# Pinning VectorE, ScalarE and GpSimd to the written order in attention and router, cutting the router into pieces, and splitting a prologue in two

## The chip, the cores and the metric

The kernel runs on one core of a Trainium2 chip. The core has five engines that work side by side, each with its own queue that it works off strictly in order: TensorE (PE in the profile; its weight loads are listed as PEld), VectorE (DVE), ScalarE (ACT), GpSimd (POOL) and SyncE (SP, which here only starts DMAs). [...] The metric is the time of one launch on the device in microseconds (us); lower is better.

## What is computed

One transformer layer over 2048 tokens of width 256, in float32: multi-head causal attention with rotated keys and queries, a residual and a layer norm, then a mixture of 16 experts (top 2) plus a shared expert, a residual and a second layer norm.

```python
q = (x @ Wq)                       # 16 heads of 16: 4 plain dims, 12 rotated by position
c_kv = x @ Wkv_down                # 64 wide
k, v = c_kv @ Wk_up, c_kv @ Wv_up  # k rotated like q
scores = where(causal, -inf, q @ k.T / 4)
x = layernorm(x + softmax(scores) @ v)
p = softmax(x @ gate_w.T);  weights, indices = top_k(p, 2)
y = sum over experts e of swiglu(x, w1[e], w3[e], w2[e]) * weight_of(e)
z = swiglu(x, sw1, sw3, sw2)       # the shared expert
out = layernorm(x + y + z)
```

## The kernel before

The tokens are cut into four chunks `c` of 512, the heads into four groups `g` of four. The name `g, c` stands for the queries of one chunk in one group.

**Attention is done in two passes.** The maxima pass (class `Maxima`) multiplies queries by keys, tile by tile, only to find each query's largest score: four matmuls per step, one a head (tiles `m`), which VectorE reduces to maxima (`pm`, lines 485 and 490). When all of `g, c` is through, `negated` (line 492) makes the tile `nm`: GpSimd fills it with zeros (line 494), VectorE writes the negated maxima into one column of 32 (line 495). `shift` (line 500) lets TensorE transpose `nm` into `pn`, and VectorE adds it to the queries, giving `qa`. The value pass (class `Weighted`) multiplies keys by `qa` (tiles `s`), ScalarE takes exponentials into `p` (line 535), GpSimd zeroes the upper triangle of diagonal tiles by an affine select (line 539), and TensorE multiplies by the values (`av`, one bank). The sums over key blocks are collected in `avs`: ScalarE copies `av` to `more` (line 566) and GpSimd adds it (line 567), or, in steps without a maxima part, VectorE adds it straight from PSUM (line 563).

**A plan written by hand sets the order.** The list `steps` pairs a maxima step with a value step; the main loop (from line 716) issues per step: two heads of `s`, two of `m`, their exponentials and reductions, then the other two heads of each, then the `av` matmuls of the step before, and then whatever `put(step, ...)` hung on this step: projections of keys, queries and values (`pk`, `pq`, `pv`), `negated` and two steps later `shift`, `finish` (line 569: divide, add to the residual, statistics), and for the last group the router. The last 20 value steps have no maxima part.

**The router of a chunk** is `normed` (layer norm, an inverse root of 12 small VectorE operations and four scalings), `turned` (transposes `pt`, copies to `xT`), `choose` (logits `lg`, softmax, top 2), `settle` (the place of each token in its expert's room, from two matmuls `pc`) and `scatter` (eight indirect DMAs, line 278, each issued by GpSimd). For the chunks 3, 0 and 1 they hang on steps at the end of attention; chunk `LAST` (2) is routed after it, between the shared expert's matmuls, and then the expert blocks follow.

**`prologue(c)`** transposes a chunk of x, copies it to `xT` and computes the latent `ckv` (`pc`) in one go; for the chunks 2 and 3 it hangs on the steps 3 and 7. `double(g)` (line 336) hangs on step 5 for g = 1 to 3: nine small copies on GpSimd, which wait for DMAs of weights (`wks`, `sines`).

**What sets an engine's order.** A scheduler at build time orders each engine's instructions by priority and readiness, by its own model of time, and may move an instruction ahead of earlier written ones. Only instructions handed to `tc.keep_in_program_order` keep the written order; before the change these are the matmuls and transposes, by the helper `pe` (line 136), and a few DMAs.

## Time and profile before

| what | value |
|---|---|
| median of 3 runs | 811.31 us (810.15 to 811.82) |
| the profiled execution, as timed | 803.1 us |
| its span, first to last instruction | 801.1 us |
| mean granted TensorE clock | 0.993 |
| busy: PE, DVE, ACT, POOL | 771.5, 547.1, 445.0, 323.0 us |
| attention with both passes | about 160 to 535 us of the span |
| last 20 value steps with three routers | about 535 to 595 us |
| shared expert, expert blocks, combination | from 595 us |

The page is read so: an engine's busy time is the union of its instructions; a matmul's end is modelled, so a busy PE says little, while the starts of matmuls are measured. In the timeline each row is a run of like instructions: start, length, engine, line, what is written and read, how many, and in brackets the idle time of the engine before it and what ended it. Every matmul of float32 has two records, a transpose one. All PE instructions stand under line 140, the helper's line, so they are told apart by their tiles.

### The profile page before, as it was taken

The page shows a single profiled execution, that of the slowest core. Times are in us where ns is not written, and L with a number is a line of the kernel's source. Part 1 is how long each engine was busy: PE and PEld are TensorE (multiplying, and loading weights), DVE is VectorE, ACT ScalarE, POOL GpSimd, SP SyncE. Part 2 cuts the span into 40 slices and gives each one's busy share as a digit, 9 for nine tenths or more (in the row PEclk, how much of TensorE's full clock was granted, in tenths as well). Part 3 has the DMA queues.
Part 4 walks back from the last instruction along what each step waited for, and adds up shares of the span by engine and source line. Part 5 has one row for each costly group of instructions (what it writes and reads, how often), then busy time and mean ns, then how long its engine had stood idle before and what let it go on. Part 6 is the DMA issues. An engine that isn't in the chain of part 4 may idle for free. (4 is left out here: it accounts for less than half of the span.)

```text
span 801.1 us, 14999 instructions
## 1 busy us (share of the span) xinstructions
PE 771.5 (96%) x5086; PEld 361.3 (45%) x5086; DVE 547.1 (68%) x1489; ACT 445.0 (56%) x997; POOL 323.0 (40%) x557
## 2 busy tenths in 40 slices
PE   7999999999999999999999999999989899999985
PEld 3443433444333344543334453444336466666543
DVE  2768888887687887777788678788775433333276
ACT  1143646377775786766688668875742033333345
POOL 2032524434355454635455454461661333333300
PEclk9999999999999999999999999999999999999998
DMA  5469999991000000001000000000225322222172
GB/s 147 130 174 327 310 301 304 294 301 54 2 1 1 1 2 1 2 19 37 1 2 2 1 2 2 1 2 2 80 84 141 107 80 86 82 86 70 37 230 85
DMA packets 67378, 71.88 MB, mean 90 GB/s; under 512 B 4736, under 2 KB 61539, under 8 KB 67302
## 3 DMA queue, kind: packets, MB, share of 16 engines
q1 hardware_dynamic: 62286, 61.77, 27.7%
q0 software_dynamic: 3552, 8.43, 3.0%
q10 hardware_dynamic: 1464, 0.72, 0.4%
q8 instruction: 41, 0.67, 0.4%
q14 instruction: 35, 0.29, 0.1%
HBM read 26.44 MB, written 45.78 MB: 90 GB/s over the span
## 5 line engine op out<-in xcount | busy, mean ns | idle before, releaser
L535 ACT ACTIVATE p<-s 128x512 f32<-128x512 f32 (+3 forms) x640 | 292.6, 540 | 128.2 <-PE m L140 79.0
L140 PE MATMUL m<-k,q 32*128 32x512 f32 (+3 forms) x1280 | 303.9, 566 | 0.8 <-DVE rot L423 0.5
L140 PE MATMUL s<-qa,k 32*128 32x512 f32 (+3 forms) x1280 | 279.4, 556 | 1.8 <-DVE avs L563 0.7
L490 DVE TENSOR_REDUCE pm<-m 128x1 f32<-128x512 f32 x384 | 237.5, 681 | 44.4 <-PE m L140 44.0
L567 POOL TENSOR_TENSOR avs<-avs,more 128x512 f32<-128x512 f32 (+3 forms) x125 | 136.7, 1094 | 167.3 <-ACT more L566 163.8
L140 PEld LDWEIGHTS s<-qa,k 32*128 32x128 f32 x1280 | 107.1, 184 | 117.6 <-ACT p L535 67.6
L140 PE MATMUL av<-p,v 128*32 128x512 f32 (+3 forms) x1280 | 154.2, 540 | 1.9 <-DVE base L244 1.2
L140 PEld LDWEIGHTS m<-k,q 32*128 32x128 f32 x1280 | 122.7, 184 | 44.5 <-issue 11.9
L485 DVE CUSTOM_DVE_ANT_0 m<-m,qmask 128x512 f32<-128x512 f32 (+3 forms) x256 | 118.3, 521 | 29.1 <-PE m L140 26.1
L566 ACT COPY more<-av 128x512 f32<-128x512 f32 (+3 forms) x125 | 65.6, 525 | 38.3 <-PE av L140 30.4
L539 POOL TENSOR_SCALAR_AFFINE_SELECT p<-p 128x128 f32<-128x128 f32 x256 | 70.5, 297 | 38.2 <-ACT p L535 36.4
L931 POOL DMA_INDIRECT yg<-yb,to x42 | 41.4, 985 | 88.2 <-ACT yb L923 44.1
L140 PEld LDWEIGHTS av<-p,v 128*32 128x32 f32 x1280 | 27.1, 108 | 104.1 <-ACT p L535 54.2
L140 PE MATMUL ph<-w,xbT 128*128 x168 | 60.3, 482 | 2.4 <-DVE xbT L884 1.7
L903 DVE TENSOR_TENSOR rh<-ru,ph 128x176 f32<-128x176 f32 x42 | 14.2, 338 | 53.7 <-ACT ru L901 53.7
L140 PE MATMUL h<-xT,cs 128*128 128x512 f32 (+1 forms) x96 | 43.6, 599 | 4.9 <-DVE sh L794 2.0
L901 ACT ACTIVATE ru<-ph 128x176 f32<-128x176 f32 x42 | 13.3, 318 | 59.3 <-PE ph L140 59.3
L140 PE MATMUL py<-w2r,hT 88*128 x168 | 43.4, 380 | 0.7 <-ACT hT L910 0.7
L278 POOL DMA_INDIRECT xg<-xr,slot x32 | 31.1, 971 | 31.1 <-issue 19.8
L140 PEld LDWEIGHTS ph<-w,xbT 128*128 128x128 f32 x168 | 28.5, 189 | 20.8 <-issue 11.6
L428 POOL TENSOR_TENSOR k<-rot 128x512 f32<-128x512 f32 x16 | 20.3, 1267 | 42.5 <-DVE rot L426 42.5
L140 PEld LDWEIGHTS py<-w2r,hT 88*128 88x128 f32 x168 | 31.7, 189 | 12.0 <-ACT hT L910 1.2
(147 smaller groups left out, 633.3 us busy)
## 6 DMA issues: line engine op xcount, KB each, us to landing
xg<-hot SPq DMA_DIRECT2D x16, 2064.0 KB
w<-in_w_dram SPq DMA_DIRECT2D x4, 1408.0 KB
xb<-xg SPq DMA_DIRECT2D x42, 129.0 KB
got<-yg SPq DMA_DIRECT2D x8, 512.0 KB
w2r<-in_w_dram SPq DMA_DIRECT2D x2, 1408.0 KB
xr<-in_x_dram SPq DMA_DIRECT2D x4, 512.0 KB
out_dram<-o SPq DMA_DIRECT2D x8, 256.0 KB
cs<-in_rope_dram SPq DMA_DIRECT2D x16, 80.0 KB
```

The costliest lines, as they stand in the source:

```text
L140: tc.keep_in_program_order(op(*args, **kw))
L278: put = nc.gpsimd.indirect_dma_start(out=xg[:, :], out_offset=bass.IndirectOffsetOnAxis(ap=slot[:, j, i : i + 1], axis=0), in_=xr[c][:, t, ...
L428: nc.gpsimd.tensor_tensor(ks[g, c], tmp[:, 0, :], tmp[:, 1, :], ALU.add)
L485: nc.vector.tensor_tensor_reduce(out=ps[:, :n], in0=ps[:, :n], in1=qmask[:, CH - n :], scale=1.0, scalar=3.0 * NEG, op0=ALU.add, op1=ALU.m ...
L490: nc.vector.tensor_reduce(to, ps, AX.X, ALU.max)
L535: nc.scalar.activation(pr[:, n0:], ps[:, n0:], AF.Exp, scale=SCALE)
L539: nc.gpsimd.affine_select(out=diag, in_=diag, pattern=[[1, P]], base=0, channel_multiplier=-1, compare_op=ALU.is_ge, fill=0.0,)
L566: nc.scalar.copy(more[:, n0:], pv[:, n0:])
L567: nc.gpsimd.tensor_tensor(to, to, more[:, n0:], ALU.add)
L901: nc.scalar.activation(u, ph[:, :INTER], AF.Silu)
L903: nc.vector.tensor_tensor(us[b], u, ph[:, INTER:], ALU.mult)
L931: nc.gpsimd.indirect_dma_start(out=yg[:, :], out_offset=bass.IndirectOffsetOnAxis(ap=to[:, 0:1], axis=0), in_=yb, in_offset=None, bounds_c ...
```

## The change

Three wrappers, `dve`, `act` and `pool`, hand every operation called through them to `keep_in_program_order`; all VectorE, ScalarE and GpSimd operations of attention and router now go through them. The functions of the router become generators that yield between pieces, and from three steps after a chunk's last value step on, up to three pieces are issued per step, with four empty pieces after each function. `prologue` loses the latent, which becomes `latent`, issued one step later for the chunks 2 and 3.

```diff
+    class InOrder:
+        def __init__(self, engine):
+            self.engine = engine
+        def __getattr__(self, name):
+            op = getattr(self.engine, name)
+            return lambda *args, **kw: tc.keep_in_program_order(op(*args, **kw))
+    dve, act, pool = InOrder(nc.vector), InOrder(nc.scalar), InOrder(nc.gpsimd)
...
         def negated(g, c):
             nm = wk1.tile([P, 4, 4, PAD], F32, tag="nm", name=f"nm{g}_{c}")
-            nc.gpsimd.memset(nm, 0.0)
-            nc.vector.tensor_reduce(
+            pool.memset(nm, 0.0)
+            dve.tensor_reduce(
...
-                nc.gpsimd.tensor_copy(w[:, :, LOW:], o[:, :, NOPE:HD])
+                pool.tensor_copy(w[:, :, LOW:], o[:, :, NOPE:HD])
...
+        def latent(c):
+            copy = act.copy if c else dve.tensor_copy
             pc = bank(f"pc{c}")
...
             if what is prologue:
                 put(step, what, c)
+                put(step + 1, latent, c)
...
+        def routed(c):
+            for work in (normed(c), turned(c, bank), choose(c, bank), settle(c, bank), scatter(c)):
+                yield from work
+                yield from (None,) * 4
+        def pieces_of(step, pieces):
+            for _ in range(3):
+                if next(pieces, "end") == "end":
+                    return
+            put(step + 1, pieces_of, step + 1, pieces)
...
             if g == G - 1:
-                put(i + 2, normed, c)
-                if c != LAST:
-                    put(i + 6, turned, c, bank)
-                    put(i + 7, lambda c=c: chosen.update({c: choose(c, bank)}))
-                    put(i + 11, lambda c=c: settle(c, bank, chosen[c]))
-                    for t in range(4):
-                        put(i + 12, scatter, c, t)
+                if c == LAST:
+                    put(i + 2, lambda c=c: at_once(normed(c)))
+                else:
+                    put(i + 3, pieces_of, i + 3, routed(c))
```

The instruction counts of every engine stay as they were (a matmul, a reduction or a DMA is neither added nor removed). In the two built programs the queues differ as follows. TensorE: `pc` of the chunks 2 and 3 stands one step later, and the router's `pt`, `lg` and `pc` one or two steps later. ScalarE: the latent's copies and three small exponentials of the router stand some places later. SyncE: nothing. GpSimd: all 16 memsets of `nm` stand later than before, each right before the reduction that needs it in the written order, that is behind the GpSimd work of the same step; the nine copies of `double` stand together ahead of the key sum of chunk 2 and the first affine selects; the 16 scatters of the chunks 3 and 0 stand together, ahead of the affine selects of the last diagonal. VectorE: two reductions into `nm` stand behind the rotations `rot` of the same step, `q` of chunk 1 stands ahead of some maxima, and in the last 70 us of attention the router's small operations and the additions to `avs` are sorted otherwise.

More of the change, by code (lines that the diff above doesn't have):

```diff
@@ L154, in inverse_root, with at_once @@
         v, guess, y = tile_("nv"), tile_("ng", I32), tile_("ny", I32)
-        nc.vector.tensor_scalar(v, var, EPS, None, ALU.add)
-        nc.vector.tensor_scalar(guess, v.bitcast(I32), 1, None, ALU.logical_shift_right)
-        nc.vector.tensor_scalar(y, guess, -1.0, float(0x5F3759DF), ALU.mult, ALU.add)
+        dve.tensor_scalar(v, var, EPS, None, ALU.add)
+        dve.tensor_scalar(guess, v.bitcast(I32), 1, None, ALU.logical_shift_right)
+        dve.tensor_scalar(y, guess, -1.0, float(0x5F3759DF), ALU.mult, ALU.add)
         y = y.bitcast(F32)
         for i in range(3):
+            yield
             a, b = tile_(f"na{i}"), tile_(f"nb{i}")
-            nc.vector.scalar_tensor_tensor(a, y, -0.5, y, ALU.mult, ALU.mult)
-            nc.vector.tensor_tensor(a, a, v, ALU.mult)
-            nc.vector.scalar_tensor_tensor(b, a, 1.5, y, ALU.add, ALU.mult)
+            dve.scalar_tensor_tensor(a, y, -0.5, y, ALU.mult, ALU.mult)
+            dve.tensor_tensor(a, a, v, ALU.mult)
+            dve.scalar_tensor_tensor(b, a, 1.5, y, ALU.add, ALU.mult)
             y = b
         return y
+    def at_once(pieces):
+        for _ in pieces:
+            pass
+    chosen = {}
     x1T = xT
     def normed(c):
-        rstd = inverse_root(mv[:, 4 * c : 4 * c + 4, 1], 4, f"ln{c}")
+        rstd = yield from inverse_root(mv[:, 4 * c : 4 * c + 4, 1], 4, f"ln{c}")
         for t in range(4):
-            nc.vector.tensor_scalar(
+            yield
+            dve.tensor_scalar(
                 xr[c][:, t, :E], xr[c][:, t, :E], mv[:, 4 * c + t, 0:1], rstd[:, t : t + 1],
@@ L179, in turned @@
         for k in range(2):
+            yield
             pt = bank(f"pt1_{c}_{k}")
@@ L182, in turned @@
                 transpose(pt[:, t * P : (t + 1) * P], xr[c][:, t, k * P : (k + 1) * P], ident)
-            nc.vector.tensor_copy(x1T[c][:, k, :], pt)
+            dve.tensor_copy(x1T[c][:, k, :], pt)
     def choose(c, bank):
+        yield
         lg = bank(f"lg{c}")[:, : 4 * NEXP].rearrange("p (t n) -> p t n", n=NEXP)
@@ L202, in choose @@
         top = small("top", 1)
-        nc.vector.tensor_reduce(top[:, :, 0], lg, AX.X, ALU.max)
+        dve.tensor_reduce(top[:, :, 0], lg, AX.X, ALU.max)
         pr = small("pr")
-        nc.vector.tensor_tensor(pr, lg, wide(top), ALU.subtract)
-        nc.scalar.activation(pr, pr, AF.Exp)
+        dve.tensor_tensor(pr, lg, wide(top), ALU.subtract)
+        yield
+        act.activation(pr, pr, AF.Exp)
+        yield
         tot = small("tot", 1)
-        nc.vector.tensor_reduce(tot[:, :, 0], pr, AX.X, ALU.add)
-        nc.vector.reciprocal(tot, tot)
-        nc.vector.tensor_tensor(pr, pr, wide(tot), ALU.mult)
+        dve.tensor_reduce(tot[:, :, 0], pr, AX.X, ALU.add)
+        dve.reciprocal(tot, tot)
+        dve.tensor_tensor(pr, pr, wide(tot), ALU.mult)
+        yield
         tiles = slice(4 * c, 4 * c + 4)
@@ L214, in first_of_largest, with settle @@
             best = gates[:, j, tiles].unsqueeze(2)
-            nc.vector.tensor_reduce(best[:, :, 0], of, AX.X, ALU.max)
+            dve.tensor_reduce(best[:, :, 0], of, AX.X, ALU.max)
             hit = small(f"hit{j}")
-            nc.vector.tensor_tensor(hit, of, wide(best), ALU.is_equal)
-            nc.vector.tensor_tensor(hit, hit, ranks, ALU.mult)
+            dve.tensor_tensor(hit, of, wide(best), ALU.is_equal)
+            dve.tensor_tensor(hit, hit, ranks, ALU.mult)
+            yield
             at = small(f"at{j}", 1)
-            nc.vector.tensor_reduce(at[:, :, 0], hit, AX.X, ALU.max)
-            nc.vector.tensor_tensor(hot[:, j, tiles, :], ranks, wide(at), ALU.is_equal)
-            return at
-        at = first_of_largest(pr, 0)
-        nc.gpsimd.tensor_copy(xr[c][:, :, E + 1 : ROW], at)
+            dve.tensor_reduce(at[:, :, 0], hit, AX.X, ALU.max)
+            dve.tensor_tensor(hot[:, j, tiles, :], ranks, wide(at), ALU.is_equal)
+            return at
+        at = yield from first_of_largest(pr, 0)
+        yield
+        pool.tensor_copy(xr[c][:, :, E + 1 : ROW], at)
         rest = small("rest")
-        nc.vector.scalar_tensor_tensor(rest, hot[:, 0, tiles, :], -2.0, pr, ALU.mult, ALU.add)
-        first_of_largest(rest, 1)
+        dve.scalar_tensor_tensor(rest, hot[:, 0, tiles, :], -2.0, pr, ALU.mult, ALU.add)
+        yield from first_of_largest(rest, 1)
+        yield
         both = small("both")
-        nc.vector.tensor_tensor(both, hot[:, 0, tiles, :], hot[:, 1, tiles, :], ALU.add)
-        return both
-    def settle(c, bank, both):
+        dve.tensor_tensor(both, hot[:, 0, tiles, :], hot[:, 1, tiles, :], ALU.add)
+        chosen[c] = both
+    def settle(c, bank):
+        yield
         tiles = slice(4 * c, 4 * c + 4)
         pc = bank(f"pc1_{c}")[:, : 8 * NEXP].rearrange("p (a t n) -> p a t n", t=4, n=NEXP)
-        every = both.rearrange("p t n -> p (t n)")
+        every = chosen[c].rearrange("p t n -> p (t n)")
         for a, w in enumerate((before, ones)):
@@ L243, in settle @@
         base = rt.tile([P, 4, NEXP], F32, tag="base", name=f"base{c}")
-        nc.vector.tensor_copy(base[:, 0, :], fill)
+        dve.tensor_copy(base[:, 0, :], fill)
         for t in range(3):
-            nc.vector.tensor_tensor(base[:, t + 1, :], base[:, t, :], pc[:, 1, t, :], ALU.add)
-        nc.vector.tensor_tensor(fill, base[:, 3, :], pc[:, 1, 3, :], ALU.add)
-        nc.vector.tensor_tensor(base, base, pc[:, 0], ALU.add)
+            dve.tensor_tensor(base[:, t + 1, :], base[:, t, :], pc[:, 1, t, :], ALU.add)
+        yield
+        dve.tensor_tensor(fill, base[:, 3, :], pc[:, 1, 3, :], ALU.add)
+        dve.tensor_tensor(base, base, pc[:, 0], ALU.add)
         of = rt.tile([P, 2, 4, NEXP], F32, tag="of", name=f"of{c}")
-        nc.vector.tensor_tensor(
+        dve.tensor_tensor(
             of, hot[:, :, tiles, :], base.unsqueeze(1).to_broadcast([P, 2, 4, NEXP]), ALU.mult
         )
+        yield
         place = rt.tile([P, 2, 4], F32, tag="place", name=f"place{c}")
-        nc.vector.tensor_reduce(place, of, AX.X, ALU.add)
-        nc.vector.tensor_copy(slot[:, :, tiles], place)
+        dve.tensor_reduce(place, of, AX.X, ALU.add)
+        dve.tensor_copy(slot[:, :, tiles], place)
     scattered = []
@@ L273, in wait_for, with scatter @@
             )
-    def scatter(c, t):
-        i = 4 * c + t
-        for j in range(2):
+    def scatter(c):
+        for i, j in ((4 * c + t, j) for t in range(4) for j in range(2)):
+            yield
             put = nc.gpsimd.indirect_dma_start(
@@ L280, in scatter @@
                 out_offset=bass.IndirectOffsetOnAxis(ap=slot[:, j, i : i + 1], axis=0),
-                in_=xr[c][:, t, :], in_offset=None,
+                in_=xr[c][:, i % 4, :], in_offset=None,
             ).ins
@@ L339, in double @@
             w = wks[g].rearrange("p (h d) -> p h d", d=PAD)
-            nc.gpsimd.tensor_copy(w[:, :, LOW:], w[:, :, NOPE:HD])
+            pool.tensor_copy(w[:, :, LOW:], w[:, :, NOPE:HD])
             for k in range(2):
@@ L400, in prologue @@
         def prologue(c):
-            copy = nc.scalar.copy if c else nc.vector.tensor_copy
+            copy = act.copy if c else dve.tensor_copy
             for k in range(2):
@@ L407, in prologue @@
                 copy(xT[c][:, k, :], pt)
+        def latent(c):
+            copy = act.copy if c else dve.tensor_copy
             pc = bank(f"pc{c}")
@@ L422, in project_k @@
                 )
-            nc.vector.scalar_tensor_tensor(
+            dve.scalar_tensor_tensor(
                 tmp[:, 0, :], pk[0], unit, cs[c][:, 0, :], ALU.add, ALU.mult
             )
-            nc.vector.tensor_tensor(tmp[:, 1, :], pk[1], cs[c][:, 1, :], ALU.mult)
+            dve.tensor_tensor(tmp[:, 1, :], pk[1], cs[c][:, 1, :], ALU.mult)
             ks[g, c] = kv.tile([P, CH], F32, tag="k", name=f"k{g}_{c}")
-            nc.gpsimd.tensor_tensor(ks[g, c], tmp[:, 0, :], tmp[:, 1, :], ALU.add)
+            pool.tensor_tensor(ks[g, c], tmp[:, 0, :], tmp[:, 1, :], ALU.add)
         def project_q(g, c):
@@ L437, in project_q @@
             qs[g, c] = wk3.tile([P, CH], F32, tag="q", name=f"q{g}_{c}")
-            nc.vector.tensor_tensor(qs[g, c], pq, cq[c], ALU.mult)
+            dve.tensor_tensor(qs[g, c], pq, cq[c], ALU.mult)
         def project_v(g, c):
@@ L452, in project_v @@
             for a in range(2):
-                nc.scalar.copy(
+                act.copy(
                     v.rearrange("p (b a m) -> p b a m", a=2, m=P)[:, :, a, :],
@@ L456, in project_v @@
                 )
-            nc.gpsimd.memset(v.rearrange("p (h d) -> p h d", d=PAD)[:, :, ONE : ONE + 1], 1.0)
+            pool.memset(v.rearrange("p (h d) -> p h d", d=PAD)[:, :, ONE : ONE + 1], 1.0)
             vs[g, c] = v
@@ L484, in reductions @@
                     if kc == self.c:
-                        nc.vector.tensor_tensor_reduce(
+                        dve.tensor_tensor_reduce(
                             out=ps[:, :n], in0=ps[:, :n], in1=qmask[:, CH - n :], scale=1.0,
@@ L489, in reductions @@
                     else:
-                        nc.vector.tensor_reduce(to, ps, AX.X, ALU.max)
+                        dve.tensor_reduce(to, ps, AX.X, ALU.max)
         def negated(g, c):
             nm = wk1.tile([P, 4, 4, PAD], F32, tag="nm", name=f"nm{g}_{c}")
-            nc.gpsimd.memset(nm, 0.0)
-            nc.vector.tensor_reduce(
+            pool.memset(nm, 0.0)
+            dve.tensor_reduce(
                 nm[:, :, :, ONE], pm[g, c][:, :, :, : c + 1], AX.X, ALU.max, negate=True
@@ L507, in shift @@
             qa[g, c] = wk3.tile([P, CH], F32, tag="qa", name=f"qa{g}_{c}")
-            nc.vector.tensor_tensor(qa[g, c], qs[g, c], pn, ALU.add)
+            dve.tensor_tensor(qa[g, c], qs[g, c], pn, ALU.add)
         class Weighted:
@@ L534, in exponentials @@
                     pr = wkp.tile([P, CH], F32, tag="pr", name=f"p{g}_{c}_{kb}_{j}")
-                    nc.scalar.activation(pr[:, n0:], ps[:, n0:], AF.Exp, scale=SCALE)
+                    act.activation(pr[:, n0:], ps[:, n0:], AF.Exp, scale=SCALE)
                     if kb >= 4 * c:
                         diag = pr[:, n0 : n0 + P]
-                        nc.gpsimd.affine_select(
+                        pool.affine_select(
                             out=diag, in_=diag, pattern=[[1, P]], base=0, channel_multiplier=-1,
@@ L558, in values @@
                     avs[g, c] = wk2.tile([P, CH], F32, tag="avs", name=f"avs{g}_{c}")
-                    nc.scalar.copy(avs[g, c], pv)
+                    act.copy(avs[g, c], pv)
                     return
@@ L562, in values @@
                 if alone:
-                    nc.vector.tensor_tensor(to, to, pv[:, n0:], ALU.add)
+                    dve.tensor_tensor(to, to, pv[:, n0:], ALU.add)
                 else:
                     more = wk2.tile([P, CH], F32, tag="more", name=f"more{g}_{c}_{kb}")
-                    nc.scalar.copy(more[:, n0:], pv[:, n0:])
-                    nc.gpsimd.tensor_tensor(to, to, more[:, n0:], ALU.add)
+                    act.copy(more[:, n0:], pv[:, n0:])
+                    pool.tensor_tensor(to, to, more[:, n0:], ALU.add)
         def finish(g, c):
@@ L575, in finish @@
             rs = wk2.tile([P, 4, 4, 1], F32, tag="rs", name=f"rs{g}_{c}")
-            nc.vector.reciprocal(rs, po[:, :, :, ONE : ONE + 1])
+            dve.reciprocal(rs, po[:, :, :, ONE : ONE + 1])
             oh = wk2.tile([P, 4, 4, HD], F32, tag="oh", name=f"oh{g}_{c}")
-            nc.vector.tensor_tensor(oh, po[:, :, :, :HD], rs.to_broadcast([P, 4, 4, HD]), ALU.mult)
+            dve.tensor_tensor(oh, po[:, :, :, :HD], rs.to_broadcast([P, 4, 4, HD]), ALU.mult)
             xg = xr[c][:, :, g * 4 * HD : (g + 1) * 4 * HD]
-            adder = nc.vector if g == G - 1 else nc.gpsimd
+            adder = dve if g == G - 1 else pool
             adder.tensor_tensor(xg, xg, oh.rearrange("p t h d -> p t (h d)"), ALU.add)
@@ L584, in finish @@
                     st = wk2.tile([P, 6], F32, tag="st", name=f"st{c}_{t}")
-                    nc.vector.bn_stats(st, xr[c][:, t, :E])
-                    nc.vector.bn_aggr(mv[:, 4 * c + t, :], st)
+                    dve.bn_stats(st, xr[c][:, t, :E])
+                    dve.bn_aggr(mv[:, 4 * c + t, :], st)
         steps = []
@@ L665, in block_kernel @@
         at = {}
-        chosen = {}
         def put(step, what, *args):
@@ L710, in block_kernel @@
         prologue(0)
+        latent(0)
         project_k(0, 0)
@@ L713, in block_kernel @@
         prologue(1)
+        latent(1)
         prior = None
@@ L977, in block_kernel @@
     shared_hidden(3, 1)
-    turned(LAST, spare)
+    at_once(turned(LAST, spare))
     shared_hidden(3, 2)
-    both = choose(LAST, spare)
+    at_once(choose(LAST, spare))
     shared_out(3)
     shared_hidden(0, 0)
-    settle(LAST, spare, both)
-    for t in range(4):
-        scatter(LAST, t)
+    at_once(settle(LAST, spare))
+    at_once(scatter(LAST))
     own, row, end, total = table()
```

## The prediction

> **What bounds the kernel now.** I read the page first, then busy times by stage, then the timeline of single engines where the order changes.

> ```profile
> PE 771.5 (96%) x5086; PEld 361.3 (45%) x5086; DVE 547.1 (68%) x1489; ACT 445.0 (56%) x997; POOL 323.0 (40%) x557
> ```
> ```profile
> 60.00:160.00 100.00, 99.83 (x666) 41.16 (x662) 84.53 (x183) 49.25 (x108) 39.60 (x69) 0.98 1.10 307
> 160.00:520.00 360.00, 359.00 (x2900) 150.15 (x2898) 282.04 (x687) 261.78 (x575) 174.14 (x299) 1.00 0.09 24
> 520.00:600.00 80.00, 75.81 (x570) 32.44 (x567) 62.22 (x248) 50.40 (x114) 40.96 (x81) 1.00 0.12 40
> ```

> PE is busy throughout attention, but its ends are modelled, so I look at starts. One step of the middle:

> ```profile
> 264.22 0.70 PE L140 MATMUL s<-qa,k 32*128 32x512 f32 x2
> ...
> 266.14 1.06 PE L140 MATMUL av<-p,v 128*32 128x512 f32 x8
> 267.14 0.70 PE L140 MATMUL s<-qa,k 32*128 32x512 f32 x2
> ...
> 269.07 1.07 PE L140 MATMUL av<-p,v 128*32 128x512 f32 x8
> 270.07 0.70 PE L140 MATMUL s<-qa,k 32*128 32x512 f32 x2
> ```

> From step to step 2.92 and 2.93 us: two quartets of s and m (0.96 each), four av (1.00). A single pair of `pq`, which uses the whole array, starts 1.91 us before the next (259.38 and 261.29 in the same timeline), 0.955 per matmul. So the quartets already run at the pace of one full matmul: in 160 to 520 PE is the bound, and time lost there isn't won back. In 60 to 160 the steps without values are paced by VectorE (four reductions at 0.61 us).

> How much slack lies between VectorE and PE? A step takes nine banks of eight (4 s, 4 m, 1 av), so a bank comes round after eight allocations. If I take each m reduction's end and the start of the matmul eight allocations later, a tenth of the pairs are within 0.06 us and half within 1.1 us. A late VectorE stops PE nearly at once.

> **The memset of `nm`, the main term.** `nm` is zeroed by GpSimd and then partly written by VectorE, so the reduction waits for the memset. It costs 526 ns (16 of them). Before, it ran long ahead:

> ```profile
> 256.45 0.53 POOL L494 MEMSET nm<- 128x512 f32 x1 [0.80 <-PE pn L140]
> ...
> 268.06 1.26 POOL L567 TENSOR_TENSOR avs<-avs,more 128x512 f32<-128x512 f32 x1 [1.66 <-ACT more L566]
> ```
> ```profile
> 265.46 2.48 DVE L490 TENSOR_REDUCE pm<-m 128x1 f32<-128x512 f32 x4 [0.44 <-PE m L140]
> 268.05 0.19 DVE L495 TENSOR_REDUCE nm<-pm 128x16 f32<-128x32 f32 x1
> 268.38 2.48 DVE L490 TENSOR_REDUCE pm<-m 128x1 f32<-128x512 f32 x4
> ```

> The memset at 256.45 is for the reduction at 268.05. Pinned, it stands behind the addition that ends at 269.33 (268.06 + 1.26), which itself waits for ScalarE's copy of the same step's av. It ends at 269.86, the reduction starts near 269.92: 1.87 us late. Queued behind it on VectorE are the reductions of the next step, whose banks PE needs two steps on. VectorE has 0.14 us idle after it, so about 1.7 us reach PE.

> I did this for all 16 (late start minus VectorE's idle time after the reduction, from the same two timelines):
> - three in the first group's maxima-only steps (60.1, 95.9, 149.2): late 2.26, 2.41, 2.39, idle 0.88, 0.86, 0.92: 4.4 us;
> - five at a change of group (195.7, 301.9, 328.5, 433.6, 462.1): late 2.97, 3.10, 2.97, 3.41, 2.97, idle 1.20, 1.37, 1.20, 1.37, 1.20: 9.1 us;
> - three like the one shown (268.1, 399.7, 523.8): late 1.87 each, idle 0.15, 0.14, 0.25: 5.1 us;
> - two (249.1, 382.0) where the rotations now go first (1.4 us of useful work) and the memset also waits for the key sum: the reduction, next at 250.7, starts at 252.7, 2.0 late, some 1.85 each: 3.7 us;
> - no cost: the first (written early), the one at 473.4 (idle 1.81 against 2.02, and `q` goes ahead of it), the one at 536.2 (counted in the tail).

> Sum 22.3 us. Bounds: 17 if the half microsecond of slack that many banks have is kept every time; 27 if late VectorE also delays `qa` and the projections.

> [...] By the measured starts, PE has no idle time to catch up with, and the sum is 22. [...]

> **The copies of `double`.**

> ```profile
> 46.99 0.22 POOL L340 COPY wks<-wks 128x48 f32<-128x48 f32 x1 [2.70 <-DMA wks<-in_wk_dram]
> ...
> 51.10 0.55 POOL L539 TENSOR_SCALAR_AFFINE_SELECT p<-p 128x128 f32<-128x128 f32 x2
> 51.73 0.22 POOL L340 COPY wks<-wks 128x48 f32<-128x48 f32 x1
> 51.90 0.55 POOL L539 TENSOR_SCALAR_AFFINE_SELECT p<-p 128x128 f32<-128x128 f32 x2
> 53.07 0.38 POOL L345 COPY wqs<-sines 128x48 f32<-128x48 f32 x2 [0.62 <-DMA sines<-in_wq_dram]
> ```

> GpSimd waits for weights that land until 53. Before, four selects slipped in at 51.10 to 52.45, and PE went on after av_0_0 at 53.48. Pinned, all nine copies end at 53.4, then the key sum of chunk 2 (1.27), then the four selects (0.27 each): 54.7 to 55.7, 3.3 us later. PE waits for them in av_0_0, and nothing later in that stage has slack, since VectorE paces it. +3.2 us. This also swallows what the later latent saves upstream (0.35 to 0.4 us of waiting for ScalarE's copies, twice) and what `q` of chunk 1, waiting for its DMA until 30.4 ahead of eight maxima, may cost (at most 1).

> **The tail, 520 to 600.** Twenty value steps of some 2.07 us (s 1.07, av 1.00) are stretched by VectorE's order:

> ```profile
> 558.39 1.14 PE L140 MATMUL s<-qa,k 32*128 32x512 f32 x8
> 559.46 1.38 PE L140 MATMUL av<-p,v 128*32 128x512 f32 x8
> 560.77 2.39 PE L140 MATMUL s<-qa,k 32*128 32x512 f32 x8
> ...
> 569.40 2.25 PE L140 MATMUL s<-qa,k 32*128 32x512 f32 x8
> 572.83 1.06 PE L140 MATMUL av<-p,v 128*32 128x512 f32 x8 [1.17 <-DVE base L244]
> ```

> At 560.77 the next start is 2.33 away, not 1.07 (an av bank isn't added until 561.3, behind eleven router operations); at 569.40 it is 3.43 (a `pc` bank is held until 572.7). With smaller ones (1.1 at 538, 1.7 at 586) the stalls sum to 8.5 us. The new order frees those two banks sooner and moves `pt` one step on: some 5 us can go. Against it: the statistics of chunk 3 (eight operations, 2.4 us) now stand whole ahead of `qa` and four maxima of the last maxima steps, +1 to 2 us; and GpSimd. Its scatters take 1.27 us each (0.97 and 0.30 between). Chunk 3's places are settled later (`pc` comes after the logits of chunk 0 and an exponential), by my count near 565 instead of 559; sixteen scatters from there end at 585.5, against 584.1 now, and only then come the selects of the last diagonal, which were ready at 585.25. So the last four steps can't start earlier, `settle` of chunk 1 now stands ahead of chunk 2's `finish`, and TensorE's h at 595.3 stays about where it is. I take 0, bounds -6 (scatters earlier than I think) and +4.

> After attention the order is the same but for two small operations: 0.

> **Sum.** 22.3 + 3.2 + 0 = 25.5 us on the profiled execution: span 801.1 to about 826.6, timed 803.1 to 828.6. The median of the runs, 811.3, lies 8.2 us above that execution; I assume the same gap: 836.8, so about 837.

> **Rivals.**
> [...]
> - *Faster*: the place is the tail. All 8.5 us of its stalls go and GpSimd's scatters are out of the way, while the memset costs nothing because the addition ahead of it ends before VectorE comes to the reduction; the latent saves 1: 811.3 - 9 + 3 = about 805. It decides at a late start under VectorE's idle time (0.14 to 1.37); measured are 1.87 to 3.41, so it is improbable.
> - *Stalls grow*: each late reduction also delays `qa` and projections, GpSimd's additions run into one another: 27 + 3 + 4 and something on top, 850.
> - *The change doesn't take place*: excluded but for small print; the built queues show the memsets behind the additions.

> **How the numbers follow.** Main case 0.70 (828 to 845); VectorE catches up 0.15 (814 to 828); stalls grow 0.08; faster 0.05; nothing 0.02. The range, 822 to 846, takes in the main case's bounds (17 to 27, tail -6 to +4) and half of the second. A difference under 0.2% (1.6 us) can't be told from none here: faster 0.05, same 0.02, slower 0.93.

> **What would show it.** Right: VectorE's reduction into `nm` idles for some 2 us each, ended by GpSimd's memset, in all about 30 us; PE starts after it lie 1.5 to 2 us beyond 2.93; the first affine selects at 54.7; the stage 160 to 520 longer by about 17. [...] The tail shows by the distance from the last maxima to h: 60 us as before if I am right.

## The result and the profile after

The changed kernel takes 847.25 us (median of 4 runs, 845.85 to 849.20) against 810.73 us (809.91 to 811.82) for the kernel before on the same chip: a ratio of 1.0451, with a 95% interval of 1.0421 to 1.0481. It is 36.5 us slower. The prediction was 837, with a range of 822 to 846, so the direction and most of the size were right, and the time lies just outside the range. The profiled execution took 848.57 us (span 846.7) at a mean granted TensorE clock of 0.962.

First the busy times of the page, then the three stages. The cuts 66.31, 168.65 and 547.14 are where the work stands that stood at 61.2, 160 and 520 before. The third row ends at 643, just behind the work that stood at 600 before, which is now at 642. The columns are stretch, length, then busy time and instructions of PE, PEld, DVE, ACT and POOL, then the granted clock of TensorE.

```profile
PE 804.0 (95%) x5086; PEld 372.3 (44%) x5086; DVE 551.1 (65%) x1489; ACT 446.9 (53%) x997; POOL 321.8 (38%) x557
```
```profile
66.31:168.65 102.34, 100.59 (x655) 41.57 (x657) 84.82 (x183) 48.81 (x107) 38.02 (x64) 0.98 1.09 303
168.65:547.14 378.49, 375.49 (x2901) 156.36 (x2897) 281.34 (x686) 263.00 (x576) 173.37 (x299) 0.98 0.06 18
547.14:643.00 95.86, 86.78 (x572) 34.84 (x569) 67.56 (x251) 51.24 (x114) 43.01 (x85) 0.89 0.14 41
```

VectorE, ScalarE and GpSimd do the same work as before (DVE 551.1 against 547.1). PE is "busy" 32.5 us longer without one more instruction. So nothing was added; the work waits, or runs at a lower clock. Measured between the same pieces of work, the first stage is longer by 3.5 us, the second by 18.5, the third by 15. The clock of the third stage is 0.89; before, it was 1.00 there.

The predicted wait is there. This is the row of VectorE's wait for the memset (total, times, longest), and then the step that the prediction worked out, the reduction that stood at 268.05:

```profile
DVE nm L156 <- POOL nm L156: 31.5, 13, 3.1
```
```profile
281.07 1.27 POOL L156 TENSOR_TENSOR avs<-avs,more 128x512 f32<-128x512 f32 x1 [1.66 <-DVE pm L156]
282.28 0.53 POOL L156 MEMSET nm<- 128x512 f32 x1
```
```profile
278.47 2.48 DVE L156 TENSOR_REDUCE pm<-m 128x1 f32<-128x512 f32 x4 [0.44 <-PE m L140]
282.84 0.19 DVE L156 TENSOR_REDUCE nm<-pm 128x16 f32<-128x32 f32 x1 [1.88 <-POOL nm L156]
282.94 4.98 DVE L156 TENSOR_REDUCE pm<-m 128x1 f32<-128x512 f32 x8
```
```profile
280.15 0.70 PE L140 MATMUL s<-qa,k 32*128 32x512 f32 x2
...
283.08 1.72 PE L140 MATMUL s<-qa,k 32*128 32x512 f32 x4
...
286.52 1.07 PE L140 MATMUL av<-p,v 128*32 128x512 f32 x8
...
288.11 0.70 PE L140 MATMUL s<-qa,k 32*128 32x512 f32 x2
```

All pinned operations now stand under line 156, the wrapper's. The memset follows the addition of its own step (282.28), VectorE idles 1.88 us (predicted 1.87), then reduces eight banks in a row without a gap (4.98 us; a bank is one of the kernel's eight tiles of 128 x 512 float32 that TensorE writes, `ps_sc`): those of the late step and of the next. PE's step from 280.15 to 283.08 is the usual 2.93; the next lasts 5.03 up to 288.11, of which the four transposes of `nm` are 0.59 (287.52 to 288.11), leaving 1.5 too many. The step after it takes 2.92 again (288.11 to 291.03), so the loss is not made up.

### The profile page after: what moved, and what is told of

It reads as the page before. It is cut to its first block, busy times and chain, and to the rows that moved or that the text cites. A ratio compares the mean times of both kernels' runs of the same rounds, so it can differ in the third digit from the quotient of the medians.

```text
span 846.7 us, 15000 instructions
## 1 busy us (share of the span) xinstructions
PE 804.0 (95%) x5086; PEld 372.3 (44%) x5086; DVE 551.1 (65%) x1489; ACT 446.9 (53%) x997; POOL 321.8 (38%) x557
## 3 DMA queue, kind: packets, MB, share of 16 engines
q1 hardware_dynamic: 62286, 61.77, 26.4%
## 5 line engine op out<-in xcount | busy, mean ns | idle before, releaser
L140 PE MATMUL m<-k,q 32*128 32x512 f32 (+3 forms) x1280 | 312.4, 574 | 4.6 <-DVE pm L156 3.1
L140 PE MATMUL s<-qa,k 32*128 32x512 f32 (+3 forms) x1280 | 293.1, 576 | 3.1 <-DVE pm L156 1.8
L140 PE MATMUL av<-p,v 128*32 128x512 f32 (+3 forms) x1280 | 160.8, 561 | 6.9 <-issue 2.5
L140 PEld LDWEIGHTS s<-qa,k 32*128 32x128 f32 x1280 | 111.4, 190 | 125.6 <-ACT p L156 65.9
L140 PEld LDWEIGHTS m<-k,q 32*128 32x128 f32 x1280 | 124.6, 186 | 52.1 <-DVE pm L156 19.2
L156 ACT COPY more<-av 128x512 f32<-128x512 f32 (+3 forms) x125 | 65.6, 525 | 37.5 <-PE av L140 29.3
L140 PEld LDWEIGHTS av<-p,v 128*32 128x32 f32 x1280 | 28.2, 109 | 113.3 <-ACT p L156 50.5
L140 PE MATMUL ph<-w,xbT 128*128 x168 | 61.8, 492 | 2.6 <-DVE xbT L931 1.6
L140 PE MATMUL h<-xT,cs 128*128 128x512 f32 (+1 forms) x96 | 45.9, 624 | 6.1 <-DVE oh L156 2.5
L140 PE MATMUL py<-w2r,hT 88*128 x168 | 43.4, 380 | 0.7 <-ACT hT L957 0.7
L140 PEld LDWEIGHTS ph<-w,xbT 128*128 128x128 f32 x168 | 29.3, 194 | 21.6 <-issue 13.0
L140 PEld LDWEIGHTS py<-w2r,hT 88*128 88x128 f32 x168 | 31.7, 189 | 12.0 <-ACT hT L957 1.2
```

The costliest lines, as they stand in the source:

```text
L140: tc.keep_in_program_order(op(*args, **kw))
L156: return lambda *args, **kw: tc.keep_in_program_order(op(*args, **kw))
```

## Where the time stands, by TensorE's starts

The table gives how much later (us) a matmul starts than in the first profile of the kernel before, at five places: first key projections (65.9), end of the maxima-only steps (152.1), last maxima steps (527.9), first matmul `h` of the shared expert (595.3), and the expert blocks (679.6). The last column is the time spent at half clock between 535 and 720 of each run's own span. Profiles are single executions, from different chips, on which the kernel before took between 805.9 and 813.1 us. Two programs can also differ by the execution alone: e9 and e10 are alike up to the last stage, and stand 5.2 us apart at 65.9. So places are read from this table, and sizes from the ratios to the kernel before on the same chip.

| kernel | ratio (95%) | 65.9 | 152.1 | 527.9 | 595.3 | 679.6 | half clock |
|---|---|---|---|---|---|---|---|
| the change | 1.0451 (1.0421 to 1.0481) | 6.3 | 7.9 | 28.6 | 40.5 | 44.6 | 23.9 |
| e1_nm_free | 1.0132 (1.0090 to 1.0174) | 4.6 | 4.6 | 4.7 | 16.5 | 21.5 | 27.3 |
| e2_double_later | 1.0382 (1.0333 to 1.0431) | 0.7 | 2.3 | 21.9 | 31.8 | 37.0 | 20.5 |
| e3_old_router | 1.0452 (1.0414 to 1.0491) | 5.3 | 10.4 | 28.5 | 44.0 | 45.6 | 23.9 |
| e4_three_undone | 1.0079 (1.0053 to 1.0105) | 0.8 | -0.2 | -0.1 | 14.9 | 17.6 | 23.9 |
| e5_before_again | 1.0004 (0.9988 to 1.0020) | -0.2 | 1.4 | 1.4 | 2.6 | 3.1 | 3.4 |
| e6_pool_only | 1.0279 (1.0240 to 1.0319) | 6.1 | 8.2 | 26.1 | 27.7 | 30.4 | 6.8 |
| e7_dve_only | 1.0213 (1.0173 to 1.0253) | 3.2 | 3.3 | 3.9 | 17.6 | 21.3 | 27.3 |
| e8_pieces_only | 1.0051 (1.0033 to 1.0070) | 1.8 | 0.8 | 0.8 | 3.1 | 5.7 | 10.2 |
| e9_two_undone | 1.0110 (1.0076 to 1.0144) | -2.1 | -0.5 | -0.5 | 9.3 | 14.7 | 20.5 |
| e10_stats_pieces | 1.0269 (1.0244 to 1.0294) | 3.1 | 2.1 | 2.8 | 29.8 | 34.2 | 37.5 |
| e11_dve_free | 1.0027 (1.0015 to 1.0039) | 3.9 | 2.9 | 2.9 | 10.1 | 11.9 | 17.1 |
| e12_stats_early | 1.0034 (1.0021 to 1.0048) | 1.5 | 1.6 | 1.4 | 9.2 | 13.0 | 20.5 |
| e13_four_pieces | 1.0120 (1.0093 to 1.0146) | -0.4 | 1.3 | 1.4 | 17.3 | 20.5 | 30.7 |
| e14_stats_six | 1.0233 (1.0206 to 1.0259) | -0.1 | -1.0 | -1.1 | 21.3 | 26.6 | 34.1 |
| e15_dve_free_five | 1.0228 (1.0201 to 1.0255) | 5.0 | 4.0 | 4.0 | 25.0 | 28.1 | 27.3 |

The row of the change shows four losses, as one execution has them. 5.1 us are lost by 60, predicted as 3.2; the other 1.2 of the 6.3 at 65.9 belong to the first late reduction. From there to 527.9 another 22 are lost, which is the memset. The 12 between the last maxima and the first `h` were predicted as 0, and so were the 4 between `h` and the expert blocks, where two half-clock windows begin (at 636.2 and 680.6).

## The experiments

The theory at this point: the memset costs some 24 us, the copies of `double` 3 to 5, and something in the last stage 7 to 12. The rivals were VectorE's own order, the pieces of the router, the prologue in two steps, and the clock. In the edits, `pool.` and `dve.` are pinned calls, `nc.gpsimd.` and `nc.vector.` free ones.

**e1_nm_free: only the memset is not pinned.**

```diff
-            pool.memset(nm, 0.0)
+            nc.gpsimd.memset(nm, 0.0)
```

> The changed kernel with one operation no longer pinned: GpSimd's memset of nm. My theory (the pinned memset makes the reduction late at 13 places, about 22 us, and the TensorE starts show some 23 of the 36.5 us between 60 and 527): 847.3 - 24 = about 823, VectorE's idle time before nm ended by GpSimd falls from about 31 us to under 8, and the half-clock windows between 160 and 520 go. Rival (VectorE's own pinned order is the cost and the memset is only the first in line, the next wait takes its place): 840 to 845.

Measured: 823.66 us, ratio 1.0132. That is 0.0319 below the change's ratio, or 26 us of 811 (about 22 to 30, from both intervals). VectorE's wait for the memset is gone from the list of waits, and the whole rise between 65.9 and 527.9 is gone with it (4.6 to 4.7). The rival, in which the next wait takes its place, falls.

**e2_double_later: the nine copies at step 8 instead of step 5.**

```diff
-            put(5, double, g)
+            put(8, double, g)
```

> The changed kernel with the copies of double for groups 1 to 3 moved from step 5 to step 8, behind the key sum of chunk 2 and the first four selects. My theory (the copies wait for weights that land until 53 and hold the selects back): 847.3 - 3 to -5 = about 843, and av of step 0 starts near 52 to 53. Rival (the loss at the start is the half-clock window there, or the two-step prologue): no difference, 847.

Measured: 841.68 us, ratio 1.0382: 5.6 us less (1 to 10). Here is why, first GpSimd in the changed kernel, then PE in the kernel before, in the changed one, and with the copies at step 8:

```profile
52.16 0.22 POOL L156 COPY wks<-wks 128x48 f32<-128x48 f32 x1 [0.53 <-DMA wks<-in_wk_dram]
53.58 0.39 POOL L156 COPY wqs<-sines 128x48 f32<-128x48 f32 x2 [1.20 <-DMA sines<-in_wq_dram]
53.93 1.26 POOL L156 TENSOR_TENSOR k<-rot 128x512 f32<-128x512 f32 x1
55.14 2.04 POOL L156 TENSOR_SCALAR_AFFINE_SELECT p<-p 128x128 f32<-128x128 f32 x8
```
```profile
51.45 2.10 PE L140 MATMUL av<-p,v 128*32 128x512 f32 x8
```
```profile
55.49 2.67 PE L140 MATMUL av<-p,v 128*32 128x512 f32 x8 [2.51 <-POOL p L156]
```
```profile
50.54 1.94 PE L140 MATMUL av<-p,v 128*32 128x512 f32 x8
```

The first selects start at 55.14 (predicted 54.7), and `av` at 55.49 instead of 51.45. Of these 4.0 us, PE had lost 2.0 by the step before, and 2.51 it stands idle in front of `av`. In the profiles of e1 and e3, which also have the copies at step 5, PE loses 3.4 and 3.5 us between the step before and `av`; with the copies at step 8 it loses nothing there. By 60 another 1.1 have gone in the change; the clock is at a half from 52.5 to 59.3.

**e3_old_router: the router as it was, not pinned and at its old steps; attention stays pinned.**

```diff
-                    put(i + 3, pieces_of, i + 3, routed(c))
+                    put(i + 2, lambda c=c: at_once(normed(c)))
+                    put(i + 6, lambda c=c: at_once(turned(c, bank)))
+                    put(i + 7, lambda c=c: at_once(choose(c, bank)))
...
```

> The changed kernel with the router as before: not pinned and at its old steps; attention stays pinned, the statistics in finish too. Theory T1 (the 12 us that the last stage lost come from the pieces: places found later, sixteen scatters ahead of the selects of the last diagonal, settle ahead of finish): 847.3 - 12 = about 835, from the last maxima to the first h 60 us as in the kernel before. Rival T2 (they come from the pinned statistics and reductions on VectorE): 843 to 847. Rival T3 (they are only the half-clock windows that earlier stalls bring): 845 to 847, with as many windows after 527.

Measured: 848.86 us, ratio 1.0452: no difference. But this does not clear the pieces, since the old router brings a loss of its own. From the last maxima step to the value step that stood at 536.8, e3 loses 6.5 us and the change 3.3; from the value step that stood at 583.3 to the first `h`, e3 loses 2.6 and the change 6.4. So T1, my own favourite, is not settled by this run. Below, the profiles show that it holds for about half of what those last four value steps lose.

**e4_three_undone: the three edits together.**

> The three edits together: memset of nm free, double at step 8, old router. If the three costs add: 847.3 - 24 - 4 - 12 = about 807 to 811, no slower than the kernel before, with the clock back at 0.99. If they share one cause (clock windows) or the rest of the pinning costs by itself: 815 to 825.

Measured: 820.07 us, ratio 1.0079. Attention up to 527.9 is back to the kernel before (-0.1), so neither ScalarE's pins nor the two-step prologue cost anything there that a profile shows. What stays sits in the last stage. There VectorE's queue in this run reads:

```profile
530.66 0.43 DVE L156 BATCH_NORM_STATS2 st<-xr 128x6 f32<-128x256 f32 x1
...
532.92 0.17 DVE L167 TENSOR_SCALAR nv_ln<-mv 128x4 f32<-128x4 f32 x1
...
536.27 1.38 DVE L194 TENSOR_SCALAR xr<-xr,mv,nb_ln 128x256 f32<-128x256 f32 x4
537.57 0.68 DVE L156 TENSOR_TENSOR qa<-q,pn 128x512 f32<-128x512 f32 x1
```

All of chunk 3's statistics and layer norm, 7 us of it, stands ahead of `qa`, for which the next value steps wait. (The layer norm is not pinned in this run; `qa` and the statistics are.) Before, `qa` came ahead of the statistics, which were strewn between the reductions:

```profile
530.17 0.68 DVE L508 TENSOR_TENSOR qa<-q,pn 128x512 f32<-128x512 f32 x1
```

**e5_before_again: all of the change undone, for a second profile of the kernel before.**

> The changed kernel with all of the change undone: the program of the kernel before, for a second profile of it (its first profiled execution took 803.1 us at a granted clock of 0.993, while its timed runs took 810 to 815 at 0.973 to 0.985). Theory C (half-clock windows after 520 belong to the usual execution of both kernels, and the first profile happened to have none): about 811 to 813, clock 0.98, windows of 15 to 25 us in all between 520 and 700, from the last maxima to the first h some 65 to 70 us. Rival (the change brings the windows): the profile again has none there, 60 us.

Measured: ratio 1.0004. Its profile has one half-clock window in the last stage (3.4 us), where the changed kernel has 24 us of them, and from 527.9 to 595.3 it loses 1.2 us. So theory C falls, as far as two profiles tell: the windows of the last stage belong to the change. But the first profile of the kernel before (803.1 us at 0.993) was a light one. Its timed runs in the first set of experiments took 810 to 815 us at clocks of 0.973 to 0.985.

**e6_pool_only, e7_dve_only, e8_pieces_only: one part of the change each, put on the kernel before.** In the first two one wrapper stays and the others go; in the third only the pieces stay:

```diff
-    dve, act, pool = InOrder(nc.vector), InOrder(nc.scalar), InOrder(nc.gpsimd)
+    dve, act, pool = nc.vector, nc.scalar, InOrder(nc.gpsimd)
```

> The kernel before with GpSimd alone pinned (VectorE, ScalarE, router and prologue as before). My theory (memset of nm 24, copies of double 5): 812 + 29 = about 840. Rival (the late reduction costs so much only because VectorE is pinned behind it; the free order puts other reductions ahead of it): 820 to 828.

> The kernel before with VectorE alone pinned. What is left over before once the three edits were undone is 7 us (820 against 813); if VectorE's order in the last stage (statistics ahead of qa and of reductions) is that: 818 to 820, with the loss after 535. Rival (ScalarE's pins or the two-step prologue): 812.

> The kernel before with the router in pieces, three a step, and nothing pinned. The old router in the changed kernel changed nothing (848.9 against 847.3), so by that: 811 to 814. Rival (pieces alone win the stalls of the last stage, and only the pins hide it): 804 to 808. Second rival (later places delay the scatters and with them the selects of the last diagonal): 818 to 822.

Measured: GpSimd alone 830.04 us (1.0279), VectorE alone 823.51 (1.0213), the pieces alone 809.99 (1.0051), with 805.87 for the kernel before on that chip. The places separate cleanly. GpSimd's pins lose 26 us before 527.9 and 1.6 in the last stage. VectorE's pins lose 13.7 in the last stage and little before it. The pieces alone lose a little and win nothing. GpSimd alone is below my 29 (it is 22.5 by the ratio). With VectorE free, the wait for the memset is 26.4 us in 14 waits instead of 31.5 in 13: the three of the maxima-only steps shrink from some 2.3 us each to 0.4 to 0.6, so the rival named there is right in a small part. VectorE alone is above my 6 to 8 (it is 17): here the router's `normed` also stands pinned at its old step, ahead of `qa`. The parts add up to 0.0543 against 0.0451 for the whole. I take it that the pieces relieve what pinning VectorE does, since they move `normed` behind `qa`; that is argued, not tried by itself.

**e9_two_undone, e10_stats_pieces, e11_dve_free, e12_stats_early: what in VectorE's order.** All four have `double` at step 8 and the memset out of the way, which in e12 is pinned but issued one step earlier. e10 and e12 take the statistics out of `finish` and put them first among the pieces, e12 with four pieces a step.

```diff
-                    dve.bn_stats(st, xr[c][:, t, :E])
-                    dve.bn_aggr(mv[:, 4 * c + t, :], st)
...
+        def statistics(c):
+            for t in range(4):
+                yield
+                st = wk2.tile([P, 6], F32, tag="st", name=f"st{c}_{t}")
+                dve.bn_stats(st, xr[c][:, t, :E])
+                dve.bn_aggr(mv[:, 4 * c + t, :], st)
...
-            for work in (normed(c), turned(c, bank), choose(c, bank), settle(c, bank), scatter(c)):
+            for work in (statistics(c), normed(c), turned(c, bank), choose(c, bank), settle(c, bank), scatter(c)):
```

> The changed kernel with the memset of nm free and double at step 8; the router in pieces and all other pins stay. If the two costs add (23.6 and 5.6 us measured one by one): 847.3 - 29 = 818, 0.9% over the kernel before, all of what is left after the last maxima start (520). If the pieces are worse or better than the old router under pins (820.1 with that): away from 818 by 3 or more.

> As the one before, and the statistics of a finished chunk taken out of finish and put at the head of the pieces, three a step, so that they no longer stand ahead of qa and of the reductions. If they are the 7 us that are left: back to the kernel before, ratio 1.000 (811). Rival (other pinned VectorE work or GpSimd's scatters hold the last stage): ratio 1.006 to 1.012, the time appears at the next wait.

> The memset free, double at step 8, and VectorE free altogether; pieces, ScalarE's and GpSimd's other pins and the two-step prologue stay. If VectorE's order is what is left: ratio 1.000 to 1.005 (the pieces alone gave 1.005). If GpSimd's order (scatters ahead of the selects of the last diagonal) is: 1.009 or more.

> A version that keeps every pin: the memset of nm issued one step earlier (behind the addition of the step before instead of its own), double at step 8, the statistics in pieces, four pieces a step. If the three places are the whole loss and the pieces can win back stalls of the last stage: 803 to 811, ratio 0.990 to 1.000. If pinning as such costs: 1.005 to 1.01.

Measured: 820.50 us (1.0110), 834.00 (1.0269), 814.08 (1.0027), 814.16 (1.0034), with 812.08 for the kernel before. Freeing VectorE takes 0.0083 away, 6.7 us (4 to 10). e11 differs from e9 in that one wrapper only, so this is the price of VectorE's order as a whole. e12 comes to nearly the same with every pin kept. But e10, which I expected at 1.000, got worse by 13 us. PE in e10, at the end of attention, shows one cause:

```profile
613.40 0.33 PE L140 MATMUL po<-ident,avs 128*128 128x128 f32 x1 [0.22 <-DVE avs L156]
622.70 0.66 PE L140 MATMUL pc<-both,before 128*128 128x64 f32 x2 [8.97 <-DVE base L156]
```

The chain of pieces, now longer by four a chunk at three a step, outlasts the value steps: `settle` of the last routed chunk runs when nothing is left to hide it, and PE, whose order is pinned too, idles 8.97 us in front of its `pc`. In the same run scatters and selects alternate on GpSimd between 592.9 and 603.9, and PE waits for the selects. So e10 can't judge the statistics.

**e13_four_pieces, e14_stats_six, e15_dve_free_five: to tell statistics from the chain's end.** e13 is e9 with `range(4)` for `range(3)`; e14 is e12 with six pieces a step; e15 is e11 with five.

> The changed kernel with the memset free, double at step 8 and four pieces a step in place of three; the statistics stay in finish, ahead of qa. If the statistics ahead of qa are the 8 us that are left (ratio 1.011 with three pieces): 1.008 to 1.012. If it is the late end of the router's chain (places, scatters, settle of the last chunk): 1.003, as with the statistics in pieces and four a step.

> The version that keeps every pin (memset a step earlier, double at step 8, statistics in pieces), with six pieces a step in place of four. If the end of the chain still decides: below 1.000, down to 0.994. If VectorE's work per step does (more router operations between the reductions and additions): 1.003 to 1.010.

> The memset free, double at step 8, VectorE free (1.0027 with three pieces a step), and five pieces a step. If the end of the chain costs in this order too: 0.995 to 1.000. If not: 1.003.

Measured: 823.04 us (1.0120), 832.12 (1.0233), 832.36 (1.0228), with 813.11 for the kernel before. With four pieces a step and the statistics ahead of `qa` the loss stays (1.0120); with them behind it, it is 1.0034. The difference is 0.0086 or 7 us (5 to 9). It cannot all be put down to the statistics' place. As pieces they take eight more places in each chunk's chain (four pieces and four empty ones), so the rest of the router comes two steps later, too. At the value step that stood at 536.8, just behind chunk 3's statistics, e13 has lost 1.9 us since the last maxima and e12 has gained 0.7: the 2.6 between them stand behind the statistics. The rest comes later, where the chain differs, too. (The two also differ in how the memset is kept out of the way, but both stand at 1.4 at 527.9.) More pieces a step are no gain: both versions lose 16 us more. GpSimd in e14, in the last diagonal:

```profile
602.89 0.30 POOL L156 TENSOR_SCALAR_AFFINE_SELECT p<-p 128x128 f32<-128x128 f32 x1
603.37 0.98 POOL L310 DMA_INDIRECT xg<-xr,slot  x1 [0.17 <-issue]
604.66 0.97 POOL L310 DMA_INDIRECT xg<-xr,slot  x1 [0.30 <-issue]
605.93 0.96 POOL L310 DMA_INDIRECT xg<-xr,slot  x1 [0.30 <-issue]
606.91 0.55 POOL L156 TENSOR_SCALAR_AFFINE_SELECT p<-p 128x128 f32<-128x128 f32 x2
```
```profile
607.27 1.31 PE L140 MATMUL av<-p,v 128*32 128x256 f32 x4 [2.75 <-POOL p L156]
```

The chain of chunk 1 is now early enough for its scatters to fall among the selects of chunk 2, and three of them cost PE 2.75 us at once. The pieces have a narrow place: too slow, and the chain is exposed after attention; too fast, and its scatters hold the selects. No version beat the kernel before; the nearest are e11 and e12, at 1.003.

## Why the prediction was nearly right, and where it failed

**The bound.** It held. PE has no time to win back: in every row of the table, what is late at 152.1 is as late at 527.9, within 0.2 us, or later. The PEld share of the second stage is 156.36 of 378.49, 41%, and did not tell that PE had no time to give: the memset cost 24 to 26 us. The 0.955 us of one 128*128 matmul, against which the prediction held the quartets, are half of the distance between these rows of the kernel before (two `pq` matmuls in two records each, 1.91 us up to the next start):

```profile
259.38 1.98 PE L140 MATMUL pq<-xT,wqs 128*128 128x512 f32 x4
261.29 0.70 PE L140 MATMUL s<-qa,k 32*128 32x512 f32 x2
```

**The memset, 22.3 us.** Right in place and nearly in total, but with two errors that cancel, which is luck. VectorE idles 31.5 us in 13 waits (predicted 13, about 30). Comparing starts with e1 step by step, each late reduction pushes PE by 1.0 to 1.6 us, 18.4 in all: less than my 22.3, most of all at the two with the rotations (1.25 and 1.1 instead of 1.85). The other 5.5 us are the clock, which the prediction left out. Here are the windows around one late reduction in the changed kernel, then the same stretch of work in e1:

```profile
345.00:349.40 4.40, 3.98 (x30) 1.64 (x28) 1.97 (x6) 3.16 (x8) 3.40 (x8) 1.00 0.00 0
349.50:356.30 6.80, 6.80 (x40) 3.53 (x36) 3.88 (x14) 2.00 (x5) 0.88 (x3) 0.50 0.00 0
356.30:360.00 3.70, 3.70 (x49) 2.10 (x42) 2.58 (x16) 2.92 (x11) 2.96 (x10) 1.00 0.01 2
```
```profile
336.00:342.90 6.90, 6.90 (x65) 3.60 (x64) 5.69 (x22) 4.78 (x14) 3.89 (x14) 1.00 0.00 1
```

At a clock of 0.50 PE gets 40 matmul records done in 6.8 us, where e1 does 65 in 6.9. Four such windows lie between 160 and 535 in the changed kernel, none in that stage in e1, and across them PE falls back by another 0.7, 1.25, 2.2 and 1.35 us.

**The copies of `double`, 3.2 us.** The mechanism was right, and so was the stall: 3.4 and 3.5 us at `av` in e1 and e3. In all three profiles about 1 us more is lost by 60, which the prediction left out; in the changed kernel the clock is at a half there from 52.5 to 59.3. By the ratio it is 5.6, with an interval (1 to 10) that takes in the 3.2.

**The tail, 0 (bounds -6 to +4).** This is the step that failed. By the ratio of e9, which has the other two costs taken out, 8.9 us are left (6 to 12); the profile of the change loses 12 between the last maxima and the first `h`. The 0 was a balance of three estimates, and each came out worse.

First, "some 5 us can go", because banks come free sooner. Nothing went: from the value step that stood at 536.8 to the one at 583.3, PE falls back from 31.9 to 34.2 us, and the pieces alone lose 4 us (e8).

Second, "the statistics of chunk 3 now stand whole ahead of `qa` and four maxima, +1 to 2 us". By the value step behind them PE has lost some 3 (28.6 to 31.9), a half-clock window included. I had their length, 2.4 us, but not what hangs on them. This is VectorE there in the changed kernel, and PE:

```profile
559.34 0.43 DVE L156 BATCH_NORM_STATS2 st<-xr 128x6 f32<-128x256 f32 x1
559.80 0.18 DVE L156 BATCH_NORM_AGGREGATE mv<-st 128x2 f32<-128x6 f32 x1
...
561.49 0.65 DVE L156 TENSOR_TENSOR qa<-q,pn 128x512 f32<-128x512 f32 x1
562.06 0.42 DVE L156 CUSTOM_DVE_ANT_0 m<-m,qmask 128x256 f32<-128x256 f32 x1
```
```profile
562.20 0.88 PE L140 MATMUL m<-k,q 32*128 32x128 f32 x4 [0.61 <-DVE qa L156]
...
564.36 3.87 PE L140 MATMUL s<-qa,k 32*128 32x512 f32 x8
568.15 0.66 PE L140 MATMUL av<-p,v 128*32 128x128 f32 x8
```

The reductions wait behind the statistics and `qa`, the next ones behind nine operations of the inverse root. PE loses 0.5 us at 562.20 and 2.6 at 568.15; `s` there takes 3.79 us from start to start, while the clock is at a half from 564.5 to 571.3.

Third, sixteen scatters from 565 to 585.5, then the selects, and `h` "stays about where it is". This is GpSimd at the end of the scatters in the kernel before, then in the changed one, and then PE in the changed one:

```profile
583.17 0.96 POOL L278 DMA_INDIRECT xg<-xr,slot  x1 [0.30 <-issue]
585.05 0.24 POOL L225 COPY xr<-at 128x4 f32<-128x4 f32 x1 [0.92 <-DVE at L220]
585.25 0.71 POOL L539 TENSOR_SCALAR_AFFINE_SELECT p<-p 128x128 f32<-128x128 f32 x2
```
```profile
599.14 1.16 POOL L310 DMA_INDIRECT xg<-xr,slot  x1 [11.88 <-DVE slot L156]
...
614.89 0.97 POOL L310 DMA_INDIRECT xg<-xr,slot  x1 [5.37 <-issue]
...
623.77 0.96 POOL L310 DMA_INDIRECT xg<-xr,slot  x1 [0.30 <-issue]
624.74 1.04 POOL L156 TENSOR_SCALAR_AFFINE_SELECT p<-p 128x128 f32<-128x128 f32 x4
```
```profile
625.10 2.58 PE L140 MATMUL av<-p,v 128*32 128x512 f32 x8 [2.54 <-issue]
...
635.89 1.77 PE L140 MATMUL h<-xT,cs 128*128 128x512 f32 x2 [2.48 <-DVE oh L156]
```

The scatters start at 599.14, after 11.88 us of waiting for `slot`, and a second gap of 5.37 us parts the two eights. Less the 28.6 us that the change is behind at its last maxima, they run from 570.5 to 596.1, not from 565 to 585.5. The selects of the last diagonal start right behind the last one, and `av` 0.36 us after them, with 2.54 us of idle time before it. Then `h` waits 2.48 us for `oh`, which stands behind `settle` of chunk 1 on VectorE; before, it waited 1.01. In these four value steps PE falls back from 34.2 to 40.5 us, half of the loss of the tail; a half-clock window (625.9 to 629.3) has part in it. The profiles of e1, e2 and e9 show the same two waits (2.2 to 2.3 and 2.5 us). In single profiles, these steps lose 0.1 with GpSimd alone pinned and the old router (e6), 3.5 with the pieces alone (e8), 6.1 in e9, and 3.3 in e11, which is e9 with VectorE free. So about half of this loss comes with the pieces, and the other half with VectorE's order.

Between 535 and 720 there are 24 us of half clock, against 0 and 3.4 in the two profiles of the kernel before. What share of the 8.9 us they are can't be read off, as stalls and windows come together.

**The base.** The sum was set against the first profiled execution and carried over "with the same gap". The two profiled executions differ by 45.5 us, the medians by 36.5, because that execution had hardly any half-clock time (6.8 us before its last window, against 17 in the second profile). The sum of the parts fits the medians (e1 and e2 take 31.5 together, singly, e9 27.7, and 8.9 remain), so this assumption moved little, but the working of the tail started from a stage at clock 1.00 throughout.

**The rivals.** "VectorE catches up" and "faster" are out. The 814 to 828 of "VectorE catches up", half of which the range took in, was the author's estimate, and no run shows it: from 152.1 to 527.9 no row of the table makes up more than 0.2 us. "Stalls grow", 850, has the nearest number, but not its mechanism: by e1 the memset costs 26 us (22 to 30), near its upper bound of 27, and the rest comes from an order that hurts in a third place.

**What stays open.** Why a short stall is followed by a window at half clock in some places and not in others. How the 8.9 us of the tail divide between the statistics, the late scatters, `settle` and the clock: the profile shows all four, and no run takes out one of them alone. And the parts alone (0.0543) exceed the whole (0.0451), which is argued above and not shown.

## What to carry to other kernels

Pinning an engine's order makes every filler operation on it (a memset, a copy that waits for a load, statistics) part of the path of whoever comes next; before pinning, write down for each what stands directly behind it and who waits for that. Price such an operation not by its length but by the stall of the engine that sets the pace: 0.5 us of memset cost 1.0 to 1.6 us thirteen times, and 2.4 us of statistics some 3. Where a chain is cut into pieces, follow it to its end, and ask what stands behind its last piece on each engine. Where an engine at its floor is stalled, add what its clock may do afterwards (here 5.5 us in four half-clock windows beside 18.4 us of stalls), and take two profiles of the kernel before, because one may be lighter than its median.
